# Gated delta rule in a post-norm decoder layer: another order for the slabs' projections, decays, values, key products and block steps

## The chip, the cores and the metric

One core of a Trainium2 chip runs the whole layer in one launch. The metric is device microseconds (us) of one execution, as the median of several runs. All data is float32.

## The reference, cut to what matters

The layer has three parts, each followed by a residual sum and a layer norm: a gated delta rule over 1024 tokens, a cross-attention over 77 context tokens, and a mixture of 8 experts. Batch 4, width 256. The change touches the delta rule alone, which has 4 heads with keys of 64 and values of 128:

```python
normed = (x - mu) * rsqrt(var + EPS) * ln_w + ln_b
q = causal_conv_silu(normed @ Wq, conv_q)     # k and v alike; 4 taps
beta = sigmoid(normed @ Wb)
g = -exp(A_log) * softplus(normed @ Wa + dt_bias)
q = l2norm(q) * HK ** (-0.5); k = l2norm(k)
def _step(S, inp):                            # over the 1024 tokens
    q_t, k_t, v_t, g_t, b_t = inp
    S = S * exp(g_t)
    v_eff = (v_t - einsum('bhk,bhkv->bhv', k_t, S)) * b_t
    S = S + k_t[..., None] * v_eff[..., None, :]
    o_t = einsum('bhk,bhkv->bhv', q_t, S)
o = o * rsqrt(mean(o * o) + EPS) * norm_w
o = o * g_out * sigmoid(g_out)                # g_out = normed @ Wg
return x + o @ Wo
```

## The kernel before

**Slabs.** The 1024 tokens are cut into 8 slabs of 128 tokens, each for all 4 batch rows. Inside a slab the recurrence is solved as a triangular system: a 128 x 128 matrix per batch row and head (16 in all), inverted, then applied to the values and to the state carried from the slab before. A slab passes through these generators and functions:

- `project` (L274): loads the slab's x (`xi`, L277), normalizes and transposes it into `nT` (L300, L304), forms beta and the decay exponent g (matmuls `pb` L317, then some twenty tiny VectorE operations L331 to L353), projects and convolves four 128-wide chunks of q and k (`convolve`, L251: matmuls L257, one ScalarE operation L267, three VectorE ones L269, in two halves, then a Silu L272), sums their squares (L362, `pss` L365, `psst` L377) and turns the cumulated decays into factors (`pd` L384, Exp L393).
- `values` (L414): the same `convolve` for four chunks of v.
- `prepare` (L422), one per batch row: GpSimd spreads g over a mask (L426), a matmul cumulates it (`pe` L432), Exp (L433), GpSimd masks it (L434), the key products `pk` (L444), and VectorE multiplies both into the matrices `bp` (L455).
- `blocks` (L464): the 32 x 32 diagonal blocks of `bp` go through DRAM to a layout with one block per partition (DMAs L477 and L480), are inverted by 31 steps of two VectorE operations each (L488 and L494), and go back through DRAM into `tt` (L498, L503).
- `invert` (L505), one per two batch rows: builds the whole inverse from the blocks (`pw` L513, `pl` L523, `pu` L539 and L546, `pl` L555, `pu` L560).
- `scan` (L564), one per batch row: transposes (L573, L576, L597), the solve and the state (`pwt` L606, `py` L624 and L632, `po` L646 and L654, `pst` L664, L673), the output's norm and gate (L681 to L701, `pg` L690), the output projection (`pot` L705, `px` L711), and the residual and layer norm (L714 to L721).

**Order.** The generators yield where they would wait. `interleave` (L191) takes one section of each in turn, and that sets the order of the program. The framework then orders each engine's instructions by this order and by when its own model finds them ready. Each engine runs its list in that order; tiles come from pools with a fixed number of buffers, PSUM from one pool of 8 banks. For slab i + 1 the loop does:

```python
    for i in range(NS - 1):
        prepared(i + 1)
        ahead = project(i + 2, made[i + 2]) if i + 2 < NS else iter(())
        interleave(*scans(i), chain(values(made[i + 1]), islice(ahead, 9)))
        interleave(*inverts(i + 1), ahead)
```

`prepared` (L732) runs the four `prepare` in two chains and then `blocks`. So the scans of slab i have the values of slab i + 1 beside them and then the first 9 sections of the projection of slab i + 2; the inversion of slab i + 1 has the rest of that projection; `prepare` has nothing beside it. All 31 steps of `blocks` stand in the program ahead of the scans.

Of the kernel before, what the change touches and what calls it, by code (L numbers as in the profile page):

```python
# [2 lines left out]

# [1 line left out]

# [98 lines left out]
def kernel(ctx: ExitStack, tc: tile.TileContext, a: dict, out: bass.AP):  # L104
# [5 lines left out]

    const = ctx.enter_context(tc.tile_pool(name="const", bufs=1))
    banks = ExitStack()
    ps_pool = [banks.enter_context(tc.tile_pool(name="ps", bufs=8, space=PSUM))]

    def bank(name, tag="bank", bufs=None):
        kw = {} if bufs is None else {"bufs": bufs}
# [128 lines left out]
    for j in range(4):  # L245
        z = wp.tile([P, H, P], F32, tag=f"pad{j}", name=f"pad{j}")
        nc.vector.memset(z, 0.0)
        padded.append(z)
    before = []

    def convolve(dst, c, nT):  # L251

        w0 = C_CONV + c * KCONV
        for j in range(2):
            pp = bank("pp")
            for kc in range(KC):
                mm(  # L257
                    pp[:, 0 : 2 * (HALO + P)],
                    lhsT=wqkv[:, kc, c * P : (c + 1) * P],
                    rhs=nT[:, kc, 2 * j : 2 * j + 2, :].rearrange("p b t -> p (b t)"),  # L260
                    start=kc == 0,
                    stop=kc == KC - 1,
                )
            yield
            pre = pp[:, 0 : 2 * (HALO + P)].rearrange("p (b t) -> p b t", b=2)
            ch = dst[:, 2 * j : 2 * j + 2, :]
            nc.scalar.activation(ch, pre[:, :, 0:P], AF.Identity, scale=cols[:, w0 : w0 + 1])  # L267
            for n in range(1, KCONV):
                nc.vector.scalar_tensor_tensor(  # L269
                    ch, pre[:, :, n : n + P], cols[:, w0 + n : w0 + n + 1], ch, ALU.mult, ALU.add  # L270
                )
        nc.scalar.activation(dst, dst, AF.Silu)  # L272

    def project(i, made):  # L274

        made["x"] = xi = slab.tile([P, B, D], F32, tag="xi", name="xi", bufs=3)
        nc.sync.dma_start(out=xi, in_=tokens(i, a["x"]))  # L277
# [75 lines left out]
        nc.vector.tensor_scalar_max(g, g, -1e30)  # L353


        kq = [slab.tile([P, 2, B, P], F32, tag=f"kq{r}", name="kq", bufs=3) for r in range(2)]
        pss = bank("pss")
        for r in range(2):
            for n in range(2):
                yield from convolve(kq[r][:, n], (1 - n) * 2 + r, nT)  # L360
                sqr = wk.tile([P, B, P], F32, tag="sqr", name="sqr", bufs=3)
                nc.scalar.activation(sqr, kq[r][:, n], AF.Square)  # L362
                yield
                o = N_ROWS + (2 * r + n) * 2 * H
                mm(  # L365
                    pss[0 : 2 * H, :],
                    lhsT=nw[:, o : o + 2 * H],
                    rhs=sqr.rearrange("p b t -> p (b t)"),
                    start=r == 0 and n == 0,
                    stop=r == 1 and n == 1,  # L370
                )
# [6 lines left out]
                pss[:, b * 2 * H : (b + 1) * 2 * H], ssT[0 : 2 * H, b, :], ident[0 : 2 * H, 0 : 2 * H]  # L378
            )
        yield  # L380

        pd = bank("pd")
        for n, m in enumerate((le, gt, ones)):
            mm(  # L384
                pd[:, n * B * H : (n + 1) * B * H],
                lhsT=m,
                rhs=g.rearrange("p b h -> p (b h)"),
                start=True,
                stop=True,
            )  # L390
        yield
        ex = slab.tile([P, 3, B, H], F32, tag="ex", name="ex")
        nc.scalar.activation(ex.rearrange("p n b h -> p (n b h)"), pd[:, 0 : 3 * B * H], AF.Exp)  # L393
        el = slab.tile([P, B, 2], F32, tag="el", name="el")
        whole = ex[:, 2].rearrange("p b (r q) -> p b r q", q=2)
        for par in range(2):
            h0 = par * HK
            nc.vector.tensor_copy(el[h0 : h0 + HK], whole[h0 : h0 + HK, :, :, par])

        qw = slab.tile([P, B, 2, H], F32, tag="qw", name="qw")  # L400
        nc.vector.tensor_copy(qw[:, :, 0, :], ex[:, 0])
        nc.vector.tensor_scalar_mul(qw[:, :, 1, :], ex[:, 0], -1.0)

        eq, rk, ik, nb, cd = (small(n) for n in ("eq", "rk", "ik", "nb", "cd"))
        both = pss[:, 0 : 2 * B * H].rearrange("p (b n h) -> p n b h", n=2, b=B)
# [3 lines left out]
        nc.gpsimd.tensor_tensor(ik, ik, bc(phalf.unsqueeze(2), [P, B, H]), ALU.pow)  # L409
        nc.vector.scalar_tensor_tensor(nb, beta, -1.0, rk, ALU.mult, ALU.mult)  # L410
        nc.vector.scalar_tensor_tensor(cd, ex[:, 1], -1.0, nb, ALU.mult, ALU.mult)
        made.update(nT=nT, kq=kq, g=g, nb=nb, cd=cd, ik=ik, eq=eq, el=el, qw=qw)

    def values(made):  # L414
        made["v"] = v = [slab.tile([P, B, P], F32, tag=f"v{c}", name="v", bufs=2) for c in range(H)]
        for c in range(H):
            yield from convolve(v[c], NQK + c, made["nT"])

    def work(name, shape, **kw):
        return wk.tile(shape, F32, tag=name, name=name, **kw)  # L420

    def prepare(i, b, made):  # L422

        g, kq = made["g"], made["kq"]
        ee = work("ee", [P, H, 2, P])
        nc.gpsimd.tensor_tensor(  # L426
            ee[:, :, 1, :], bc(le.unsqueeze(1), [P, H, P]), bc(g[:, b, :].unsqueeze(2), [P, H, P]), ALU.mult
        )
        yield

        pe = bank("pe")
        mm(pe, lhsT=gt, rhs=ee[:, :, 1, :], start=True, stop=True)  # L432
        nc.scalar.activation(ee[:, :, 0, :], pe.rearrange("p (h t) -> p h t", h=H), AF.Exp)  # L433
        nc.gpsimd.tensor_tensor(  # L434
            ee[:, :, 1, :], ee[:, :, 0, :], bc(nge.unsqueeze(1), [P, H, P]), ALU.mult
        )
        yield

        bp = made["bp"]
        pks = [bank("pk") for par in range(2)]  # L440
        for r in range(2):
            for par, pk in enumerate(pks):
                h0 = slice(par * HK, (par + 1) * HK)
                mm(  # L444
                    pk[:, r * 2 * P : (r + 1) * 2 * P],
                    lhsT=kq[r][h0, 0, b, :],
                    rhs=kq[r][h0, :, b, :],
                    start=True,
                    stop=True,
                )  # L450
# [12 lines left out]

    def blocks(i, made):  # L464

        n = NQ * B * H
        mine = slice((i % 2) * n, (i % 2 + 1) * n)

        def diagonal(x, j):
            return x[j * Q : (j + 1) * Q, :, j * Q : (j + 1) * Q]  # L470

        def kept(x, j):
            r0 = (i % 2) * n + j * B * H
            return x[r0 : r0 + B * H, :].rearrange("h (s t) -> s h t", s=Q)

        for j in range(NQ):
            nc.sync.dma_start(out=kept(ab, j), in_=diagonal(made["bp"][:, 0], j))  # L477
        am = slab.tile([P, Q, Q], F32, tag="am", name="am", bufs=1)
        for half in range(2):
            nc.sync.dma_start(  # L480
                out=am[half * n : (half + 1) * n].rearrange("p s t -> p (s t)"), in_=ab[mine, :]
            )
        ut = slab.tile([P, Q // 2, Q], F32, tag="ut", name="ut", bufs=1)
        pr = slab.tile([P, Q // 2, Q], F32, tag="pr", name="pr", bufs=1)
        nc.sync.dma_start(out=ut.rearrange("p r t -> p (r t)"), in_=a["narrow"][:, N_UNIT:])
        for k in range(Q - 1):
# [7 lines left out]
            nc.vector.tensor_tensor(  # L494
                ut[:, :r, k + 1 :], ut[:, :r, k + 1 :], pr[:, :r, :w], ALU.add
            )
        for half in range(2):
# [231 lines left out]
        nc.gpsimd.memset(tt, 0.0)  # L729
        tts.append(tt)  # L730

    def prepared(i):  # L732
# [3 lines left out]
        interleave(*(chain(*gens[n::2]) for n in range(2)))  # L736
        blocks(i, made[i])

    def inverts(i):
        return [invert(b, made[i]) for b in range(0, B, 2)]  # L740
# [3 lines left out]
            chain(scan(i, b, made[i]), scan(i, b + 1, made[i])) for b in range(0, B, 2)  # L744
        ]

    interleave(project(0, made[0]))
    prepared(0)
    interleave(values(made[0]), project(1, made[1]))
    interleave(*inverts(0))  # L750
    for i in range(NS - 1):
        prepared(i + 1)
        ahead = project(i + 2, made[i + 2]) if i + 2 < NS else iter(())
        interleave(*scans(i), chain(values(made[i + 1]), islice(ahead, 9)))
        interleave(*inverts(i + 1), ahead)
    proj_scope.close()
    w_scope = ExitStack()
    xkv = w_scope.enter_context(tc.tile_pool(name="xkv", bufs=1, side="right"))
# [687 lines left out]
```

## Time and profile before

| | |
|---|---|
| median of 3 runs | 1990.59 us (1987.02 to 1990.92) |
| the profiled execution | 1989.58 us, of which the span is 1987.8 us |
| delta rule in the span | 0 to about 877 us |
| first transposes of the scans of slabs 0, 4, 5, 6, 7 (L573) | 140.1, 554.2, 657.6, 761.1, 827.1 us |
| TensorE, VectorE, ScalarE, GpSimd busy in one such distance (450.7 to 554.2) | 89.5, 66.6, 53.5, 24.5 of 103.5 us |
| granted TensorE clock, whole span | 0.909 |

How to read what follows: PE is TensorE (a float32 matmul of this kernel shows as two records), PEld its weight loads, DVE VectorE, ACT ScalarE, POOL GpSimd, SP the engine that issues most DMAs. PEclk is the granted clock of TensorE as a share of full speed. In the view of windows a row is one stretch of the span: its length, then each engine's busy time with its count of instructions, then PEclk, the DMA engines' share and GB/s. In a timeline a row is start, length, engine, line, operation, output and inputs, count, and in brackets the idle time before it and what ended it.

### The profile page before, as it was taken

How to read it: one execution, taken by the hardware profiler on the slowest of the kernel's cores; microseconds unless marked ns; L12 is line 12 of the kernel's file. 1: busy time of each engine (PE TensorE's matmuls, PEld its weight loads, DVE VectorE, ACT ScalarE, POOL GpSimd, SP SyncE). 2: the span in 40 equal slices, each digit the busy share in tenths (PEclk: the TensorE clock that was granted, in tenths of full speed). 3: DMA queues.
4: the chain of work that ended last, by engine and by line, in shares of the span. 5: the costliest groups of instructions: out<-in, count | busy, mean ns of one | idle time of the engine just before them, and what ended most of it. 6: DMA issues, size and time to landing. Idle time of an engine off the chain costs nothing.

```text
span 1987.8 us, 27920 instructions
## 1 busy us (share of the span) xinstructions
PE 1640.0 (83%) x9524; PEld 1163.7 (59%) x9524; DVE 1119.5 (56%) x3199; ACT 918.3 (46%) x2161; POOL 549.5 (28%) x503
## 2 busy tenths in 40 slices
PE   4678898979898888878899999999739999999900
PEld 2456575747575666744676777767616666666600
DVE  4748584857576767434466666566534444444444
ACT  3435463636464545332687776766412222222212
POOL 2222222131222222132345545555410000000065
PEclk9879898989898999789999999999869999999955
DMA  3011010110101011030401100100162111111144
GB/s 113 17 32 23 20 35 17 28 27 22 32 22 33 22 22 44 17 113 0 169 12 33 42 23 32 43 33 22 33 239 77 46 46 46 48 43 48 32 147 136
DMA packets 118347, 98.97 MB, mean 50 GB/s; under 512 B 57803, under 2 KB 106303, under 8 KB 117951
## 3 DMA queue, kind: packets, MB, share of 16 engines
q1 hardware_dynamic: 107135, 75.66, 13.0%
q0 software_dynamic: 6144, 16.79, 2.7%
q10 hardware_dynamic: 4928, 4.74, 0.7%
q8 instruction: 78, 1.28, 0.3%
q14 instruction: 62, 0.51, 0.1%
HBM read 62.12 MB, written 35.03 MB: 49 GB/s over the span
## 4 chain that ended last, share of the span: by engine, by line
PE 49%; DVE 22%; ACT 11%; POOL 8%; issue 5%; DMA 5%; SPq 0%; ACTq 0%; POOLq 0%; DVEq 0%
PE pgt L1299 6%; PE pup L1299 6%; PE pdn L1326 6%; ACT sc L1006 4%; PE pp L257 3%; DMA part<-yg,found 2%; DVE kq L269 2%; DVE v L269 2%; PE pe L432 2%; PE pxo L1040 2%; PE pss L365 2%; DVE bp L455 2%; DVE ut L494 2%; PE pmh L1317 2%; POOL xg L1145 2%
## 5 line engine op out<-in xcount | busy, mean ns | idle before, releaser
L1006 ACT ACTIVATE sc<-sc,ntop,rq 128x77 f32<-128x77 f32 x512 | 182.2, 440 | 71.0 <-DVE ntop L1004 48.2
L1352 POOL DMA_INDIRECT part<-yg,found x64 | 61.3, 958 | 454.7 <-issue 443.7
L1040 PE MATMUL pxo<-vo,aT 128*128 128x256 f32 (+1 forms) x640 | 168.4, 396 | 3.7 <-ACT aT L1025 2.8
L1308 ACT ACTIVATE sge<-sge 128x512 f32<-128x512 f32 x71 | 44.7, 630 | 247.8 <-DVE sge L1307 247.8
L257 PE MATMUL pp<-nT,wqkv 128*128 128x262 f32 x512 | 143.3, 413 | 0.0
L1299 PE MATMUL pgt<-wall,mxT 128*128 x284 | 135.5, 600 | 1.8 <-ACT mxT L1288 1.8
L1299 PE MATMUL pup<-wall,mxT 128*128 x284 | 134.8, 597 | 0.0
L1326 PE MATMUL pdn<-wdn,mhT 128*128 x568 | 134.2, 379 | 0.0
L1040 PEld LDWEIGHTS pxo<-vo,aT 128*128 128x128 f32 (+1 forms) x640 | 117.9, 199 | 21.5 <-ACT aT L1025 5.8
L963 POOL TENSOR_TENSOR rq<-rq,nhalf 128x8 f32<-128x8 f32 x64 | 106.0, 1656 | 76.1 <-DVE rq L962 73.5
L949 PE MATMUL pq<-xwq,xT 128*128 128x512 f32 x256 | 123.0, 603 | 0.5 <-ACT xT L943 0.5
L1011 POOL TENSOR_TENSOR sc<-sc,den 128x616 f32<-128x616 f32 x64 | 77.9, 1218 | 160.7 <-DVE den L1010 77.6
L269 DVE SCALAR_TENSOR_TENSOR v<-pp,cols,v 128x256 f32<-128x256 f32 x192 | 91.3, 476 | 43.9 <-ACT v L267 42.0
L269 DVE SCALAR_TENSOR_TENSOR kq<-pp,cols,kq 128x256 f32<-128x256 f32 x192 | 90.5, 478 | 45.3 <-ACT kq L267 42.8
L257 PEld LDWEIGHTS pp<-nT,wqkv 128*128 128x128 f32 x512 | 96.1, 201 | 33.2 <-issue 16.8
L989 PE MATMUL psc<-kbd,qT 128*128 128x154 f32 x512 | 93.0, 305 | 27.1 <-DVE sc L996 21.9
L1307 DVE TENSOR_TENSOR sge<-pgt,ball 128x512 f32<-128x512 f32 x71 | 49.1, 692 | 112.9 <-PE pgt L1299 112.9
L1326 PEld LDWEIGHTS pdn<-wdn,mhT 128*128 128x128 f32 x568 | 102.5, 190 | 11.0
L685 POOL TENSOR_TENSOR so<-so,nhalf 128x4 f32<-128x4 f32 x32 | 32.4, 1011 | 276.0 <-DVE so L684 276.0
L989 PEld LDWEIGHTS psc<-kbd,qT 128*128 128x128 f32 x512 | 74.6, 196 | 43.3 <-DVE sc L996 30.1
L1299 PEld LDWEIGHTS pup<-wall,mxT 128*128 128x128 f32 x284 | 54.6, 192 | 69.0 <-issue 69.0
L455 DVE SCALAR_TENSOR_TENSOR bp<-pk,nb,ee 128x256 f32<-128x256 f32 x128 | 51.7, 476 | 69.9 <-PE pk L444 40.0
(285 smaller groups left out, 3700.8 us busy)
## 6 DMA issues: line engine op xcount, KB each, us to landing
yg<-my SPq DMA_DIRECT2D x71, 128.0 KB, 1.7
mx<-xg SPq DMA_DIRECT2D x67, 128.0 KB, 2.0
xs<-xd SPq DMA_DIRECT2D x13, 512.0 KB, 4.5
xi<-in_x SPq DMA_DIRECT2D x8, 512.0 KB, 4.1
am<-ab SPq DMA_DIRECT2D x16, 256.0 KB, 4.0
xd<-kd SPq DMA_DIRECT2D x32, 128.0 KB, 2.4
wall<-in_L_ffn_gate_w SPq DMA_DIRECT2D x8, 512.0 KB, 10.5
wall<-in_L_ffn_up_w SPq DMA_DIRECT2D x8, 512.0 KB, 10.8
```

Of the source, the lines that this page charges most:

```text
L257: mm(pp[:, 0 : 2 * (HALO + P)], lhsT=wqkv[:, kc, c * P : (c + 1) * P], rhs=nT[:, kc, 2 * j : 2 * j + 2, :].rearrange("p b t -> p (b t)"), ...
L269: nc.vector.scalar_tensor_tensor(ch, pre[:, :, n : n + P], cols[:, w0 + n : w0 + n + 1], ch, ALU.mult, ALU.add)
L455: nc.vector.scalar_tensor_tensor(bp[:, :, b * H + h], pk[:, r * 2 * P : (r + 1) * 2 * P].rearrange("p (n t) -> p n t", n=2), made["nb"][:, ...
L949: mm(pq, lhsT=t["xT"][:, kc, :], rhs=xwq[:, kc, c0 : c0 + HH * XD], start=kc == 0, stop=kc == KC - 1,)
L963: nc.gpsimd.tensor_tensor(rq, rq, nhalf[:, :HH], ALU.pow)
L989: mm(ps[:, c * 2 * SC : (c + 1) * 2 * SC], lhsT=qT[:, 2 * g + c, :], rhs=kbd[:, half * XC // 2 + 2 * g + c, b, :], start=True, stop=True,)
L1006: nc.scalar.activation(sc[:, h], sc[:, h], AF.Exp, scale=rq[:, h : h + 1], bias=ntop[:, h : h + 1])
L1011: nc.gpsimd.tensor_tensor(sc, sc, bc(den.unsqueeze(2), [P, HH, SC]), ALU.mult)
L1040: mm(px[:, 0:D], lhsT=aT[:w, c, :], rhs=vo[:w, b, half * NV + c, :], start=half == 0 and c == 0, stop=half == 1 and c == NV - 1,)
L1299: mm(ps, lhsT=t["xT"][:, c, :], rhs=wall[:, bass.ds(e * EW + off + c * FF, FF)], start=c == 0, stop=c == KC - 1,)
L1326: mm(px[:, 0:D], lhsT=t["hT"][:, f, :], rhs=wdn[:, bass.ds(e * EV + f * D, D)], start=f == 0, stop=f == FC - 1,)
L1352: nc.gpsimd.indirect_dma_start(out=g, out_offset=None, in_=yg, in_offset=bass.IndirectOffsetOnAxis(ap=found[:, i, b, k : k + 1], axis=0),)
```

## The change

The diff, cut to its core:

```diff
-    ps_pool = [banks.enter_context(tc.tile_pool(name="ps", bufs=8, space=PSUM))]
+    ps_pool = [banks.enter_context(tc.tile_pool(name="ps", bufs=7, space=PSUM))]
...
-    before = []
+    before, exps = [], []
     def convolve(dst, c, nT):
...
-        nc.scalar.activation(dst, dst, AF.Silu)
-    def project(i, made):
+    def decays(i, made):
         made["x"] = xi = slab.tile([P, B, D], F32, tag="xi", name="xi", bufs=3)
...
+        pd = bank("pd")
...
+        ex = slab.tile([P, 3, B, H], F32, tag="ex", name="ex")
+        exps.append(
+            nc.scalar.activation(ex.rearrange("p n b h -> p (n b h)"), pd[:, 0 : 3 * B * H], AF.Exp)
+        )
...
+    def project(i, made):
+        nT, beta, ex = made["nT"], made["beta"], made["ex"]
         kq = [slab.tile([P, 2, B, P], F32, tag=f"kq{r}", name="kq", bufs=3) for r in range(2)]
-        pss = bank("pss")
+        pss = bank("pss", "pss", 1)
         for r in range(2):
             for n in range(2):
                 yield from convolve(kq[r][:, n], (1 - n) * 2 + r, nT)
+                nc.scalar.activation(kq[r][:, n], kq[r][:, n], AF.Silu)
...
     def values(made):
         for c in range(H):
             yield from convolve(v[c], NQK + c, made["nT"])
+        with ExitStack() as behind:
+            for e in exps:
+                behind.enter_context(tc.issue_after(e.ins))
+            exps.clear()
+            for c in range(H):
+                nc.scalar.activation(v[c], v[c], AF.Silu)
...
     def prepare(i, b, made):
-        nc.scalar.activation(ee[:, :, 0, :], pe.rearrange("p (h t) -> p h t", h=H), AF.Exp)
+        exps.append(
+            nc.scalar.activation(ee[:, :, 0, :], pe.rearrange("p (h t) -> p h t", h=H), AF.Exp)
+        )
...
     def blocks(i, made):
         nc.sync.dma_start(out=ut.rearrange("p r t -> p (r t)"), in_=a["narrow"][:, N_UNIT:])
+        yield
+        yield
         for k in range(Q - 1):
...
+            if k % 3 == 2:
+                yield
...
-    for i in range(NS - 1):
-        prepared(i + 1)
-        ahead = project(i + 2, made[i + 2]) if i + 2 < NS else iter(())
-        interleave(*scans(i), chain(values(made[i + 1]), islice(ahead, 9)))
-        interleave(*inverts(i + 1), ahead)
+    interleave(decays(0, made[0]))
+    interleave(project(0, made[0]), decays(1, made[1]))
+    interleave(*prepares(0))
+    interleave(blocks(0, made[0]), project(1, made[1]))
+    for i in range(NS):
+        gens = [*inverts(i)]
+        if i + 1 < NS:
+            gens += prepares(i + 1)
+        if i + 2 < NS:
+            gens.append(decays(i + 2, made[i + 2]))
+        interleave(*gens, values(made[i]))
+        gens = [blocks(i + 1, made[i + 1])] if i + 1 < NS else []
+        if i + 2 < NS:
+            gens.append(project(i + 2, made[i + 2]))
+        if i + 1 < NS:
+            interleave(*gens, *scans(i))
```

`project` is cut in two. `decays` has its first part (x, the norm, beta, g) and the cumulated decays (`pd`, `ex`); the new `project` has the convolutions of q and k and their sums of squares. A turn of the loop now has two stretches. In the first, the inversion of slab i runs beside the key products of slab i + 1, the decays of slab i + 2 and the values of slab i, in this order within each round. In the second, the steps of `blocks` of slab i + 1 and the projection of slab i + 2 run beside the scans of slab i; both stand ahead of the scans in each round, and `blocks` has become a generator that yields twice after its loads and then after every third step. The Silus of the four chunks of v come together at the end of `values`, and `issue_after` puts them on ScalarE's list behind every Exp of the decays and key products traced since the last time (an order of issue, no wait). The sums of squares `pss` get a PSUM bank of their own; the other tiles share 7 instead of 8. The arithmetic stays the same.

More of the change, by code (lines that the diff above doesn't have):

```diff
@@ L1 @@
 from contextlib import ExitStack
-from itertools import chain, islice
+from itertools import chain
 import numpy as np
@@ L353, in project @@
         nc.vector.tensor_scalar_max(g, g, -1e30)
+        pd = bank("pd")
+        for n, m in enumerate((le, gt, ones)):
+            mm(
+                pd[:, n * B * H : (n + 1) * B * H],
+                lhsT=m,
+                rhs=g.rearrange("p b h -> p (b h)"),
+                start=True,
+                stop=True,
+            )
[4 more added lines that the diff above has]
+        )
+        el = slab.tile([P, B, 2], F32, tag="el", name="el")
+        whole = ex[:, 2].rearrange("p b (r q) -> p b r q", q=2)
+        for par in range(2):
+            h0 = par * HK
+            nc.vector.tensor_copy(el[h0 : h0 + HK], whole[h0 : h0 + HK, :, :, par])
+        qw = slab.tile([P, B, 2, H], F32, tag="qw", name="qw")
+        nc.vector.tensor_copy(qw[:, :, 0, :], ex[:, 0])
+        nc.vector.tensor_scalar_mul(qw[:, :, 1, :], ex[:, 0], -1.0)
+        made.update(nT=nT, g=g, beta=beta, ex=ex, el=el, qw=qw)
+    def project(i, made):
+        nT, beta, ex = made["nT"], made["beta"], made["ex"]
         kq = [slab.tile([P, 2, B, P], F32, tag=f"kq{r}", name="kq", bufs=3) for r in range(2)]
-        pss = bank("pss")
+        pss = bank("pss", "pss", 1)
         for r in range(2):
@@ L380, in project, with small @@
         yield
[L382 to L402, printed above, removed]
+        def small(name):
+            return slab.tile([P, B, H], F32, tag=name, name=name)
         eq, rk, ik, nb, cd = (small(n) for n in ("eq", "rk", "ik", "nb", "cd"))
@@ L411, in project @@
         nc.vector.scalar_tensor_tensor(cd, ex[:, 1], -1.0, nb, ALU.mult, ALU.mult)
-        made.update(nT=nT, kq=kq, g=g, nb=nb, cd=cd, ik=ik, eq=eq, el=el, qw=qw)
+        made.update(kq=kq, nb=nb, cd=cd, ik=ik, eq=eq)
     def values(made):
@@ L432, in prepare @@
         mm(pe, lhsT=gt, rhs=ee[:, :, 1, :], start=True, stop=True)
-        nc.scalar.activation(ee[:, :, 0, :], pe.rearrange("p (h t) -> p h t", h=H), AF.Exp)
+        exps.append(
+            nc.scalar.activation(ee[:, :, 0, :], pe.rearrange("p (h t) -> p h t", h=H), AF.Exp)
+        )
         nc.gpsimd.tensor_tensor(
@@ L496, in blocks @@
             )
+            if k % 3 == 2:
+                yield
         for half in range(2):
@@ L730, with prepares @@
         tts.append(tt)
-    def prepared(i):
+    def prepares(i):
         made[i]["bp"] = slab.tile([P, 2, B * H, P], F32, tag="bp", name="bp", bufs=2)
@@ L735, in prepared @@
         gens = [prepare(i, b, made[i]) for b in range(B)]
-        interleave(*(chain(*gens[n::2]) for n in range(2)))
-        blocks(i, made[i])
+        return [chain(*gens[n::2]) for n in range(2)]
     def inverts(i):
@@ L745, in scans @@
         ]
[L747 to L750, printed above, removed]
-    for i in range(NS - 1):
-        prepared(i + 1)
-        ahead = project(i + 2, made[i + 2]) if i + 2 < NS else iter(())
-        interleave(*scans(i), chain(values(made[i + 1]), islice(ahead, 9)))
-        interleave(*inverts(i + 1), ahead)
+    interleave(decays(0, made[0]))
[14 more added lines that the diff above has]
+            interleave(*gens, *scans(i))
     proj_scope.close()
```

## The prediction

> **What bounds the kernel now.** I read the page first: engines, slices, the chain of work that ended last.
>
> ```profile
> PE 1640.0 (83%) x9524; PEld 1163.7 (59%) x9524; DVE 1119.5 (56%) x3199; ACT 918.3 (46%) x2161; POOL 549.5 (28%) x503
> PE   4678898979898888878899999999739999999900
> PEclk9879898989898999789999999999869999999955
> PE 49%; DVE 22%; ACT 11%; POOL 8%; issue 5%; DMA 5%; SPq 0%; ACTq 0%; POOLq 0%; DVEq 0%
> ```
>
> TensorE is the busiest engine, but in slices 1 to 18, the delta rule, it falls to 8 and 7 and its clock to 7 and 8, which it does not in the experts behind. VectorE holds 22% of the chain. So the delta rule is TensorE work broken by waits. The distance between the scans of one slab and the next is 103.5 us six times over (140.1 to 761.1). The view of windows cuts one of them at 515.4 and 554.2, where the inversion and the scans begin, and adds two stretches from the end:
>
> ```profile
> 515.40:554.20 38.80, 30.87 (x313) 18.51 (x311) 19.95 (x59) 16.67 (x32) 11.58 (x9) 0.82 0.08 22
> 554.20:618.90 64.70, 58.57 (x377) 45.90 (x376) 48.65 (x164) 37.90 (x92) 12.95 (x15) 0.97 0.14 30
> 761.10:809.50 48.40, 43.57 (x288) 34.76 (x286) 37.66 (x122) 26.56 (x64) 10.55 (x11) 1.00 0.16 45
> 827.10:877.00 49.90, 44.97 (x298) 35.14 (x296) 16.16 (x44) 24.23 (x67) 10.70 (x11) 0.95 0.03 7
> ```
>
> The second column is TensorE's busy time. The stretch of inversion and key products (38.8 us) is the poor one, at clock 0.82. TensorE's timeline shows where:
>
> ```profile
> 529.46 1.15 PE L257 MATMUL pp<-nT,wqkv 128*128 128x262 f32 x4
> 535.49 1.88 PE L365 MATMUL pss<-sqr,nw 128*8 128x512 f32 x2 [4.88 <-ACT sqr L362]
> 538.03 0.59 PE L377 MATMUL psst<-sq,ssT 8*128 8x8 f32 x4 [0.67 <-ACT ssT L374]
> 538.55 1.46 PE L384 MATMUL pd<-g,sq 128*128 128x16 f32 x6
> 539.85 3.76 PE L432 MATMUL pe<-ee,sq 128*128 128x512 f32 x4
> 543.54 2.99 PE L444 MATMUL pk<-kq 64*128 64x256 f32 x16
> 548.61 3.64 PE L432 MATMUL pe<-ee,sq 128*128 128x512 f32 x4 [2.08 <-POOL ee L426]
> ```
>
> From 530.5 TensorE waits 4.88 us for the projection's tail, then runs at half speed (PEclk 0.50 from 536 to 544): four `pe` records take 3.76 us, where the start of the span, at clock 1.00, shows 1.89. Then GpSimd and VectorE hold it in `prepare`.
>
> **The work at full clock.** From start-to-start distances at clock 1.00, per slab: scans 40.6 us (transposes L573 and L576 3.6; L597 and L606 3.8; `py` 7.1; `po` and `pst` 10.1; `pg` 6.9; `pot` 2.2; `px` 6.9); v convolutions 7.15 (32 records at 0.89 per four); q and k the same; `pss` and `psst` 4.3; inversion 8.7; key products 7.8 (`pe` 3.8, `pk` 4.0); decays 3.4. Together 79.1 us of 103.5. The 38.8 us hold 24.1 of it (inversion, key products, half the q and k convolutions, 3/4 of `pss`, `psst`, `pd`), so TensorE is filled to 62%. The 64.7 us hold 55.0: 85%. Scans with values alone, 761.1 to 809.5, hold 47.75 in 48.4: 98%. The inversion with convolutions beside it (515.4 to 530.5) holds about 14.7 in 15.1: 97%.
>
> **The change, part by part.** No arithmetic is removed; two stretches are filled anew.
>
> First stretch, TensorE: inversion 8.7 + key products 7.8 + decays 3.4 + values 7.15 = 27.0 us. VectorE: inversion 5.2, `bp` 16 x 0.40 = 6.4, decays 6.2, values 24 x 0.40 = 9.6: 27.4. The 10.5 us between 530.5 and 543.6 in which the projection's tail stood alone go, since that tail now lies beside the scans, and `prepare`'s GpSimd products (8 x 1.04 to 1.27 us) have matmuls beside them. What is late next is VectorE, as full as TensorE, and the decays' chain, since the load of x waits for a buffer that the scans before release last (L714): DMA 4.1, statistics 1.8, power 1.0, four normalizations 2.1, transposes and `nT` 2.1, `pb` 1.7, some twenty tiny VectorE operations with an Exp 3.8, `pd` 1.0, Exp 0.2: 17.8 us. Behind its Exp come the table load (1.28) and four Silus (2.1), and behind those `pv` and `vt` of the scans: 21.2 us, covered by 27 while nothing stretches it; each us beyond some 30 counts in full. The floor is 27.4; the ceiling is today's 38.8, as nothing is added to its chain but VectorE work. Between fills of 62% and 97% I take the middle, 80%: 27.0 / 0.80 = **34 us**.
>
> GpSimd's products now run beside the decays' tiny operations. The trace shows such a pair:
>
> ```profile
> 574.28 1.27 POOL L701 TENSOR_TENSOR og<-og,sqr 128x512 f32<-128x512 f32 x1 [1.06 <-ACT sqr L698]
> 574.43 1.20 DVE L494 TENSOR_TENSOR ut<-ut,pr 128x56 f32<-128x56 f32 x1
> ```
>
> The VectorE operation, 0.21 us elsewhere, took 1.20 us and ended with GpSimd's; so did L348 (1.06 against 0.17). Eight products can cost 0 to 8 us; I take 2, since the `bp` and convolution rows keep 0.40 us beside GpSimd, and they are within the 34.
>
> Seven shared banks instead of eight, and six generators in turn: the first stretch asks for 36 banks in 34 us. From 515.4 to 530.5 it was 16 in 15.1 us, `pss` holding one of the eight, at 97% fill and clock 1.00. So the banks cost 0; if every `pk` had to wait for `bp`, about 5 us (two rounds of 2.4), kept for the range. A rule speaks against this: the Trainium skill, "TensorE: Matmul & The Clock Gate", section "A second HAM failure mode: psum-queue depth-cycling", reports that going through the PSUM banks can leave small gaps that throttle the clock again and again. At half clock throughout, the 27.0 us would be 54, and nothing would be gained; the row at clock 1.00 speaks for the other side, and I follow it.
>
> ScalarE changes tables four times a period (1.28 us each, at L272, L330, L698, L393). The Silus behind the Exps leave two. That saves 2.6 us of an engine that is busy 53.5 of 103.5: 0 to 2.6 on the path, counted 0. The Trainium skill, "ScalarE: Activation LUTs", section "What ACT_TABLE_LOAD costs", adds a drain of 1.38 us to each, which would make it 5.3 us. Here the Silu starts at once:
>
> ```profile
> 564.68 1.28 ACT L272 ACT_TABLE_LOAD   x1
> 565.97 0.63 ACT L272 ACTIVATE v<-v 128x512 f32<-128x512 f32 x1
> ```
>
> Second stretch, TensorE: scans 40.6 + projection 11.4 = 52.0 us. VectorE: block steps 17.0, convolutions 9.6, scans 16.6: 43.2. The projection takes the place of the values as filler, with a Square, `pss` and `psst` more; its tail, bare today, has the later scans beside it. Its cover ends with its 14th section of 17 rounds, so the scans' own tail (`og`, `pot`, `px`; 3.4 us idle between 501.8 and 507) stays. The last scans, with no filler at all, take 49.9: that and 52.0 / 0.98 = 53 are floors. Between 85% and 98% I take 91%: **57 us**.
>
> The block steps keep their number. Three every round from the third puts the last into round 13 of 17, some 44 us in; the loads land at about 13, so they do not bind. After the last step, before slab 7, it took 7.8 us until `pw` (L494 at 805.3, `pw` at 813.1): 52 us, 5 before the stretch ends. SP's list carries the same DMAs; a late store of blocks would hold the loads of x and the stores of results behind it (2.0 us at 809.15). Cost 0, up to 3 us.
>
> **The sum.** A period is 34 + 57 = 91 us: six times 12.5 = 75 us less. At the start, today's scans of slab 0 begin 26 us after `pw` (114.1 to 140.1); now a whole first stretch stands there, 36 us from a cold clock: +10. At the end the values of slab 7 (7.15 us) and their Silus lie beside an inversion that takes 14.0 us for 8.7 of work: +5; the key products of slab 7 have no decays beside them: -2. All: -62 us. On the profiled execution, 1989.58 us, that is 1927.6; on the median, 1.0 above it, **1928.6 us**.
>
> **Rivals.** *The scans wait behind the filler (slower).* Convolutions and block steps now stand ahead of the scans in every round, and VectorE takes its list in order. Were all of their 26.6 us to land on the scans' chain, the second stretch would be 49.9 + 26.6 = 76.5, the period 110.5, the time 1990.6 + 42 + 13 = 2046. It decides from a period of 101.3, a second stretch of 67.3: two thirds of the 26.6. For it: at 481.58 and 586.86 TensorE waits 1.44 us for VectorE's `qk`, with block steps around. Against it: from 761.1 to 809.5 VectorE did all 62 steps and 24 convolution operations in 48.4 us, and TensorE lost nothing.
>
> *The first stretch, or the blocks, eat a part.* If the decays' chain or VectorE keeps the first stretch at 38.8 (or the blocks come 5 us too late), the period is 95.8, the time 1990.6 - 46 + 13 = 1958. For it: in the old order that chain took from 521.4 to 532.1 for its statistics alone, since its operations stood last. Against it: it had no use to hurry there.
>
> *It does not do what it says.* If the order planned leaves TensorE's waits where they are, 1990. Against it: TensorE's list follows the program's rounds in the stretch of the inversion.
>
> *Better filled.* At 97% in both, but VectorE's 27.4 + 2 in the first: 29.4 + 53 = 82.4, the time 1990.6 - 127 + 13 = 1877.
>
> **How the numbers follow.** The forecast, periods from 86 to 97 (1899 to 1965), 0.50; a part eaten 0.18; better 0.08; no effect 0.06; slower 0.18. Within 0.2% is about what a measurement of this kernel can tell from no change. Faster 0.76, same 0.06, slower 0.18. The range from 1880 to 1995 leaves out half of the better case and most of the slower one.
>
> **What would show it.** Right: scans of successive slabs (L573) begin some 91 us apart; no idle time of 4.88 us at `pss`; `pe` near 1.9 us per four; PEclk 0.95 or more; two table loads a period; `pw` waiting for no DMA. Wrong: a first stretch above 39 us with VectorE full or `pv` waiting for Silus; TensorE waiting for `qk`, state or `og` behind L269 and L488; TensorE waiting for banks, its clock near 0.7.

## The result, and the profile after

The changed kernel takes **2043.74 us** (median of 4 runs, 2040.71 to 2045.66) against 1990.76 us of the kernel before (4 runs, 1987.02 to 1993.76): a ratio of **1.0265**, 95% interval 1.0249 to 1.0281. It is slower by 53 us; forecast were 62 us less. The profiled execution took 2045.66 us with a span of 2043.9 us. Line numbers below are those of the kernel that each line comes from; the change has moved them (the scans' first transposes: L573 before, L596 after).

The page of the changed kernel, the same four rows as in the prediction:

```profile
PE 1649.7 (81%) x9524; PEld 1177.9 (58%) x9524; DVE 1123.3 (55%) x3199; ACT 905.3 (44%) x2149; POOL 549.8 (27%) x503
PE   4569697878878798886989999999829999999910
PEclk9869798888979699998999999999959999999965
PE 52%; DVE 19%; ACT 9%; POOL 8%; DMA 6%; issue 5%; SPq 0%; ACTq 0%; POOLq 0%; DVEq 0%
```

VectorE's share of the chain fell from 22% to 19%, as wished, and TensorE's rose from 49% to 52%; but in the slices of the delta rule TensorE's busy share still alternates between 6 and 9 tenths. The scans of successive slabs now begin at 156.55, 270.24, 382.80, 495.48, 608.11, 720.72, 807.59 and 879.29 us. (In the table of the kernel before, two of these times are put too late: TensorE's timeline has the first L573 of slab 5 at 657.11 and that of slab 6 at 755.62, not 761.1, so there were five periods of 103.4 us on average and one of 98.5.) The difference of 56.1 us between the spans is made up thus: the start +16.5 (156.55 against 140.06); five full periods of 112.8 us instead of 103.4, +47.1; the period from slab 5 to slab 6, 86.9 against 98.5, -11.6; the last one, 71.7 against 71.5, +0.2; what follows, +3.9.

The view of windows, cut again where the inversion (`pw`) and the scans begin: a full turn of the loop, and then the turn in which slab 6 is inverted. The columns are length, busy time of PE, PEld, DVE, ACT and POOL with counts, PEclk, DMA share, GB/s.

```profile
558.87:608.11 49.24, 36.55 (x347) 27.38 (x346) 25.60 (x82) 18.80 (x35) 10.16 (x10) 0.72 0.06 17
608.11:671.51 63.40, 54.61 (x337) 39.93 (x336) 42.40 (x139) 33.29 (x85) 14.38 (x14) 0.97 0.14 30
783.97:807.59 23.62, 23.44 (x313) 17.86 (x312) 18.06 (x45) 13.64 (x25) 8.04 (x8) 1.00 0.04 13
807.59:862.10 54.51, 47.20 (x298) 36.33 (x297) 33.26 (x112) 25.33 (x69) 10.28 (x11) 0.91 0.15 30
```

The first stretch takes 49.2 us, where the forecast had 34 and a ceiling of 38.8. The second takes 63.4 where it had 57. The third row is the key: it is the same first stretch without the decays, since there is no slab 8, and it takes 23.6 us at clock 1.00 with TensorE busy for 23.4. That is the 27.0 us of the prediction less the 3.4 of the decays, filled to 99%. So neither seven shared banks, nor the values as filler, nor VectorE's work without the decays slow this stretch. What slows it comes with the decays.

TensorE's timeline in the full first stretch shows where; in brackets is the idle time before, and who ended it:

```profile
558.87 1.91 PE L536 MATMUL pw<-sq,tt 128*128 128x128 f32 x16
568.66 0.48 PE L299 MATMUL pt<-sq,nrm 128*128 128x128 f32 x1 [7.88 <-ACT nrm L292]
573.30 3.78 PE L449 MATMUL pe<-ee,sq 128*128 128x512 f32 x4
591.37 1.44 PE L357 MATMUL pd<-g,sq 128*128 128x16 f32 x6 [4.82 <-DVE g L352]
594.67 3.67 PE L583 MATMUL pu<-tt,wt 64*64 64x64 f32 x32
598.27 3.46 PE L449 MATMUL pe<-ee,sq 128*128 128x512 f32 x4
```

Behind the first 16 `pw` stands `pt`, the decays' transposes, and TensorE waits 7.88 us for it. Convolutions of v (L257), the next step of the inversion (`pl`) and the first key products (`pe`) stand behind it on the same list; the copies of `pw` that `pl` reads ended at 561.3, and TensorE runs through all of these without a gap as soon as `pt` is there. Later the same happens once more at `pd`, 4.82 us. After each wait four `pe` take 3.5 to 3.8 us; at full clock, at 122.76 in the same trace, they take 1.99. The chain of work that ended last, at the same place, names what the first wait waits for:

```profile
559.38 0.42 DVE kd L737
...
560.51 4.19 DMA xi<-in_x
...
566.76 1.02 POOL rs L187
...
568.01 0.61 ACT nrm L292
...
568.66 0.48 PE pt L299
```

L737 is the residual sum at the very end of the scans of the slab three before; it is the last reader of one of the three buffers `xi`. The load of x cannot start until it is done, and the program has put the use of that load at the head of the next stretch. The first turn of the loop shows the same list without that cause, since its buffer of x has never been used before: there `pt` follows `pw` without a wait, and the first stretch (116.97 to 156.55) takes 39.6 us, with the wait at `pd` alone.

```profile
120.22 0.60 PE L299 MATMUL pt<-sq,nrm 128*128 128x128 f32 x4
```

The windows between these waits show the clock:

```profile
558.87:560.80 1.93, 1.91 (x17) 1.67 (x15) 1.50 (x5) 1.07 (x2) 0.40 (x1) 1.00 0.00 0
568.66:577.00 8.34, 8.34 (x77) 5.03 (x78) 2.29 (x5) 4.92 (x8) 0.91 (x1) 0.50 0.01 2
578.50:585.00 6.50, 6.50 (x142) 5.55 (x142) 5.47 (x13) 2.10 (x6) 1.10 (x2) 1.00 0.01 3
591.37:601.00 9.63, 9.63 (x46) 7.09 (x47) 3.31 (x9) 1.28 (x3) 0.00 (x0) 0.50 0.01 2
602.50:608.11 5.61, 5.61 (x33) 4.56 (x33) 4.28 (x11) 4.10 (x7) 2.25 (x2) 1.00 0.00 1
```

After each wait TensorE works without a gap at clock 0.50, over the 8.3 and 9.6 us of these rows. So the excess of the stretch over its 27.0 us of work, 22.2 us, is the two waits (7.88 + 4.82 = 12.7) and the half clock behind them (busy 36.55 less 27.0, 9.5).

In the second stretch one wait in the scans' tail has grown: at `pot` TensorE waited 1.61 us before (at 503.44), and now 2.87. GpSimd's timeline and TensorE's show it:

```profile
547.70 2.90 POOL L419 TENSOR_TENSOR ik<-ik,phalf 128x16 f32<-128x16 f32 x1 [1.25 <-DVE rk L418]
550.55 1.26 POOL L724 TENSOR_TENSOR og<-og,sqr 128x512 f32<-128x512 f32 x1
551.87 0.66 PE L728 MATMUL pot<-sq,og 128*128 128x128 f32 x4 [2.87 <-POOL og L724]
553.96 5.08 PE L734 MATMUL px<-wo,qk 128*128 128x256 f32 x16
```

The projection's square root `ik`, a power on a tiny tile that takes 2.90 us, now stands on GpSimd's list ahead of the scans' gate `og`. TensorE waits for that `og`, and the 16 `px` behind it take 5.08 us instead of the 3.62 of full clock.

### The profile page after: what moved, and what is told of

Its sections match the earlier page's. It is cut to its first block, busy times and chain, and to the rows that moved or that the text cites. A ratio compares the mean times of both kernels' runs of the same rounds, so it can differ in the third digit from the quotient of the medians.

```text
span 2043.9 us, 27909 instructions
## 1 busy us (share of the span) xinstructions
PE 1649.7 (81%) x9524; PEld 1177.9 (58%) x9524; DVE 1123.3 (55%) x3199; ACT 905.3 (44%) x2149; POOL 549.8 (27%) x503
## 4 chain that ended last, share of the span: by engine, by line
PE 52%; DVE 19%; ACT 9%; POOL 8%; DMA 6%; issue 5%; SPq 0%; ACTq 0%; POOLq 0%; DVEq 0%
PE pgt L1330 6%; PE pup L1330 6%; PE pdn L1357 6%; ACT sc L1037 4%; PE pp L257 4%; PE pe L449 2%; DMA part<-yg,found 2%; PE px L734 2%; PE pxo L1071 2%; DVE v L269 2%; DVE bp L474 2%; PE pq L980 2%; DMA xi<-in_x 2%; POOL og L724 2%; PE pmh L1348 2%
## 5 line engine op out<-in xcount | busy, mean ns | idle before, releaser
L257 PE MATMUL pp<-nT,wqkv 128*128 128x262 f32 x512 | 152.4, 430 | 0.2 <-DVE tt L574 0.2
L257 PEld LDWEIGHTS pp<-nT,wqkv 128*128 128x128 f32 x512 | 100.0, 212 | 31.7 <-issue 11.0
L1020 PE MATMUL psc<-kbd,qT 128*128 128x154 f32 x512 | 94.0, 308 | 27.3 <-DVE sc L1027 22.2
L1357 PEld LDWEIGHTS pdn<-wdn,mhT 128*128 128x128 f32 x568 | 102.5, 190 | 11.0
L269 DVE SCALAR_TENSOR_TENSOR v<-pp,cols,v 128x256 f32<-128x256 f32 x192 | 87.0, 478 | 13.4 <-ACT v L267 11.3
L1340 DVE TENSOR_TENSOR pup<-pup,ball 128x512 f32<-128x512 f32 x71 | 49.7, 700 | 73.4 <-PE pup L1330 73.4
```

The costliest lines, as they stand in the source:

```text
L257: mm(pp[:, 0 : 2 * (HALO + P)], lhsT=wqkv[:, kc, c * P : (c + 1) * P], rhs=nT[:, kc, 2 * j : 2 * j + 2, :].rearrange("p b t -> p (b t)"), ...
L269: nc.vector.scalar_tensor_tensor(ch, pre[:, :, n : n + P], cols[:, w0 + n : w0 + n + 1], ch, ALU.mult, ALU.add)
L1020: mm(ps[:, c * 2 * SC : (c + 1) * 2 * SC], lhsT=qT[:, 2 * g + c, :], rhs=kbd[:, half * XC // 2 + 2 * g + c, b, :], start=True, stop=True,)
L1340: nc.vector.tensor_tensor(pu, pu, ball[:, bass.ds(e * FF + B_U, FF)], ALU.add)
L1357: mm(px[:, 0:D], lhsT=t["hT"][:, f, :], rhs=wdn[:, bass.ds(e * EV + f * D, D)], start=f == 0, stop=f == FC - 1,)
```

## The experiments

**The theory** behind them: the first stretch is slow because TensorE's list puts the decays' `pt` and `pd` ahead of the work that should cover their chain, and x, which begins that chain, is loaded too late; a wait costs its length and then some 4 to 5 us of half clock. **The rivals**: the filler ahead of the scans holds them up (the slower rival of the prediction); the Silus gathered at the end of the values, or the block steps in pieces, hold something up.

**An early x, and three parts undone.** In the first kernel the scans load the residual's rows a second time, so that `xi` is free as soon as its own slab is normalized:

```diff
-        made["x"] = xi = slab.tile([P, B, D], F32, tag="xi", name="xi", bufs=3)
+        made["x"] = xi = slab.tile([P, B, D], F32, tag="xi", name="xi", bufs=2)
...
+        xr = slab.tile([P, D], F32, tag="xr", name="xr", bufs=4)
+        nc.sync.dma_start(out=xr, in_=tokens(i, a["x"])[:, b, :])
...
-        nc.vector.scalar_tensor_tensor(x1, made["x"][:, b, :], 2.0, px[:, 0:D], ALU.mult, ALU.add)
+        nc.vector.scalar_tensor_tensor(x1, xr, 2.0, px[:, 0:D], ALU.mult, ALU.add)
```

> The changed kernel, except that the scans load the 128 rows of x for the residual a second time (32 small loads more), so that the buffer of a slab's x is free after its normalization and the load for the decays no longer waits for the end of the scans two slabs before. Theory A (the load of x comes late and TensorE's list has the decays' transposes ahead of the inversion, so it stands idle 7.9 us after the first transposes of the inversion and runs on at half clock): the wait of 7.9 us goes, and most of the half clock behind it; distance between scans 112.6 to about 98 us, time 1950 to 1975. Theory B (the scans wait behind convolutions and block steps on VectorE): no change, 2035 to 2050. Theory C (the Silus of v are held behind the Exps): no more than 2 us a slab, 2030 to 2045.

Measured: 1994.37 us (10 runs), ratio to before 1.0024 (1.0014 to 1.0034). The period falls from 112.6 to 102.5 us. One turn in the view of windows:

```profile
426.61:464.71 38.10, 33.25 (x347) 25.66 (x346) 23.56 (x73) 17.94 (x35) 9.12 (x9) 0.82 0.05 15
464.71:529.39 64.68, 56.05 (x337) 41.35 (x336) 42.23 (x139) 33.39 (x85) 14.39 (x14) 0.95 0.15 34
```

All of the gain lies in the first stretch (49.2 to 38.1 us), and TensorE no longer waits at `pt`. The gain is smaller than expected (1950 to 1975), since `pd` still waits for g, 4.82 us in this turn and 6.46 in the first three. The early x is worth 49 us.

The second kernel puts the scans ahead of the filler in every round:

```diff
-            interleave(*gens, *scans(i))
+            interleave(*scans(i), *gens)
```

> The changed kernel with the scans ahead of the block steps and the projection in each round of the second stretch. Theory A: nothing but a shift, 2035 to 2055, the wait before the decays' transposes still 7 to 8 us. Theory B: the second stretch of 63.4 us gets 5 to 6 us shorter, time about 2005 to 2015. Theory C: no change.

Measured: 2045.2 us (4 runs), ratio 1.0276 (1.0257 to 1.0296), no different from the change. Its second stretch takes 64.7 us, not less than the 63.4, and its `pt` still waits (7.94 us). So the filler ahead of the scans costs nothing here; the rival falls, though its price (2046) is the time that came out.

The third lets the Silus of v come when they are ready; they still stand together:

```diff
-        with ExitStack() as behind:
-            for e in exps:
-                behind.enter_context(tc.issue_after(e.ins))
-            exps.clear()
-            for c in range(H):
-                nc.scalar.activation(v[c], v[c], AF.Silu)
+        for c in range(H):
+            nc.scalar.activation(v[c], v[c], AF.Silu)
```

> The changed kernel without the order that puts the four Silus of v behind every Exp; they still stand together at the end of the values. Theory A: no change within 10 us, as the wait comes at the start of the stretch. Theory B: no change. Theory C: the transposes of v come earlier by 2 to 4 us a slab, time 2015 to 2030; against that stand up to two table loads more a slab (1.28 us each).

Measured: 2044.89 us (4 runs), ratio 1.0279 (1.0261 to 1.0297). Between 380 and 610 us ScalarE loads a table 13 times instead of 4, and nothing changes: the order of the Silus neither harms nor helps while TensorE waits for something else.

The fourth issues the steps of the blocks in one piece:

```diff
-            if k % 3 == 2:
-                yield
```

> The changed kernel with the 31 block steps issued in one piece again (the two yields behind the loads stay). Theory A: within 10 us of 2044, since the inverted blocks land 10 us before the inversion already. Theory B: if the steps in front of the scans cost time, it shows here as well, as all 62 now stand ahead of the scans from the third round on: 2050 to 2070. Theory C: no change.

Measured: 2046.09 us (4 runs), ratio 1.028 (1.0262 to 1.0297). The pieces are not what costs.

**The second wait.** Two more yields ahead of `pd` move it two rounds later, behind other sections; once on top of the early x, once on the change alone:

```diff
+        yield
+        yield
         pd = bank("pd")
```

> The second load of x for the residual, as in the run with x loaded twice (1994.4 us), and two more yields ahead of the decays' matmul pd, so that it stands behind the inversion's last products and the next key products. Theory A, continued (what is left of the loss in the first stretch is pd, which waits 4.82 us in TensorE's list for g, and the half clock of pu and pe behind it): both go, the distance between scans falls from 102.7 to about 94 us, time 1935 to 1950. Rival D (VectorE is full in this stretch, so another wait takes the place of this one at once): 1985 to 2000.

> The changed kernel with the two yields ahead of pd, without the second load of x. Theory A with two waits that add up (late x 49 us, pd 35 us): about 2008 us, with the wait of 7.9 us before the decays' transposes still there. If the late x alone makes pd late, so that pd costs nothing once it has been moved or everything comes later anyway: 2035 to 2045.

Measured on top of the early x: 1958.93 us (4 runs, 1956.73 to 1967.92), ratio 0.9848 (0.9808 to 0.9887), between what the theory and the rival expected; `pd` still waits 3.44 us. On the change alone: 2027.77 us (4 runs), ratio 1.0164 (1.0149 to 1.018), again between the two; there `pt` still waits 7.81 us and `pd` 3.44. The first stretch of each:

```profile
404.75:437.62 32.87, 29.40 (x347) 23.07 (x346) 26.42 (x78) 17.52 (x35) 10.07 (x10) 0.95 0.12 28
435.63:481.80 46.17, 34.92 (x348) 26.28 (x347) 27.91 (x88) 18.38 (x35) 11.12 (x11) 0.78 0.14 35
```

Both waits are real and separate: the early x is worth 49 us, the later `pd` 16, both together 85 (by the ratios to the kernel before, 48, 20 and 83). Why the two give some 15 to 20 more together than singly is open.

**The early x in the kernel before.** To see whether the second load would be a gain in any case, the same edit as in the first experiment was made in the kernel before:

> The kernel before with the second load of x for the residual and nothing else. If the early x helps only where the decays stand beside the inversion: 1985 to 1995, no change. If the old kernel too loses by its late x (its normalizations stood ahead of the last Square of the projection, for which TensorE waited 4.88 us): 1950 to 1975.

Measured: 1983.17 us (9 runs, 1976.78 to 1990.61), ratio 0.996 (0.9939 to 0.9981); its wait at `pss` falls from 4.88 to 3.44 us. That is 7 us against 49. The load itself did not come later by the change: before, too, it started as soon as its buffer was free (515.50, at the end of the scans of slab 3). But the first instruction on TensorE's list that needs it stood beside the next scans, 69 us later:

```profile
584.81 0.60 PE L300 MATMUL pt<-sq,nrm 128*128 128x128 f32 x4
```

In the changed kernel `pt` has its turn right behind the first 16 `pw`, 0.3 us after the load has started (560.78 against 560.51). So the wait comes from the earlier use of the load, which the change made, and not from a later load.

**The power ahead of the gate.** A first try delayed the projection's small operations by three yields, on the early x, and with the later `pd`:

```diff
         yield
+        yield
+        yield
+        yield
         def small(name):
```

> The second load of x, and three more yields ahead of the small operations at the end of the projection, so that GpSimd's power of 2.90 us stands behind the scans' last products og instead of ahead of them. If that power costs the scans' tail its wait (2.86 us at pot, and px at 4.74 instead of 3.62 us): 3 to 4 us a slab, time 1968 to 1978. If the tail is bound otherwise: 1990 to 1998.

> Second load of x, pd two yields later and the projection's small operations three yields later, together. Theory A with both: distance about 90 us, time 1915 to 1930, faster than either kernel. Rival D: 1970 or more.

Measured: 1994.42 us (10 runs), ratio 1.0017 (0.9998 to 1.0036), and 1962.42 us (4 runs, 1954.83 to 1971.49), ratio 0.9864 (0.9813 to 0.9915). Each is the same as without the yields (1968 to 1978 and 1915 to 1930 were expected), and this is inconclusive: in the trace the power (2.90 us, at 515.14) still stands ahead of `og` (518.00), and TensorE still waits 2.86 us at `pot`. The edit did not move what it was to move. A second try, on the early x with the later `pd`, gives the order itself:

```diff
-        nc.gpsimd.tensor_tensor(ik, ik, bc(phalf.unsqueeze(2), [P, B, H]), ALU.pow)
+        with ExitStack() as behind:
+            for e in ogs:
+                behind.enter_context(tc.issue_after(e.ins))
+            ogs.clear()
+            nc.gpsimd.tensor_tensor(ik, ik, bc(phalf.unsqueeze(2), [P, B, H]), ALU.pow)
...
-        nc.gpsimd.tensor_tensor(og, og, sg, ALU.mult)
+        ogs.append(nc.gpsimd.tensor_tensor(og, og, sg, ALU.mult))
```

> The run with x loaded twice and pd two yields later (1958.9 us), with GpSimd's power of the projection (2.90 us) put on its list behind the scans' two products og. In that run it stood ahead of them, TensorE waited 2.86 us for pot and ran px at 4.53 instead of 3.62 us. If the power is what holds the scans' tail: 3 to 4 us a slab, time 1930 to 1942. If the tail is bound by its own chain: 1955 to 1962.

Measured: 1941.43 us (5 runs, 1934.88 to 1946.89), ratio **0.9742** (0.9729 to 0.9756). Its windows:

```profile
393.48:427.47 33.99, 30.52 (x348) 24.05 (x346) 25.36 (x77) 17.52 (x35) 10.09 (x10) 0.90 0.15 34
427.47:485.43 57.96, 52.41 (x337) 38.64 (x336) 41.08 (x134) 33.40 (x86) 13.41 (x13) 1.00 0.12 27
```

The second stretch falls from 63.05 us in the kernel without this edit to 57.96, at clock 1.00; the waits at `pot` at its end are 0.38 and 1.00 us instead of 2.86 and 0.71, and 16 `px` take 3.62 us. So some 5 us of this stretch hung on the place of one 2.90 us instruction on GpSimd's list; the first stretch gives 1.1 of them back (32.87 to 33.99), and the five full periods fall from 96.4 to 92.3 us on average.

**One step further, and the scans first once more**, both on this last kernel. The first has two more yields ahead of `pd`, four in all; the second has the scans ahead of the filler, as in the second experiment.

> The fastest run so far (x twice, pd two yields later, the power behind og) with pd two yields later still. There pd still waits 3.44 us for g, at the end of the first stretch, and a half clock follows it. If that wait is only a matter of place: 2 to 5 us a slab less, ratio to the kernel before about 0.962 instead of 0.974. If the Exp behind pd then holds the Silus of v and with them the scans: ratio 0.975 to 0.99.

> The fastest run so far with the scans ahead of the block steps and the projection in each round of the second stretch. Theory B (convolutions and block steps on VectorE hold the scans), now that the first stretch no longer hides it: second stretch 58 us down to 53 to 55, ratio about 0.96. Theory A, that this order costs nothing: ratio 0.97 to 0.98, second stretch 57 to 60 us.

Measured with the later `pd`: **1922.36 us** (4 runs, 1920.63 to 1923.89), ratio **0.9664** (0.9643 to 0.9685), faster than both kernels. Its windows, and `pd` in TensorE's timeline:

```profile
390.22:419.71 29.49, 27.89 (x347) 21.83 (x346) 24.52 (x73) 16.46 (x33) 10.08 (x10) 1.00 0.09 23
419.71:481.52 61.81, 55.87 (x337) 41.16 (x336) 40.88 (x138) 34.55 (x88) 13.38 (x13) 0.94 0.15 33
```

```profile
417.20 0.81 PE L361 MATMUL pd<-g,sq 128*128 128x16 f32 x6 [1.57 <-DVE g L352]
```

The first stretch is down to 29.5 us for 27.0 us of work, at clock 1.00. Much of this comes back in the second (57.96 to 61.81 us): `pv` now waits 1.70 us for v's Silu at its head, and the clock there is 0.66 from 424.4 to 430.0 us. Over the five full periods the mean falls from 92.3 to 90.5 us. With the scans first: 1953.54 us (4 runs), ratio 0.9821 (0.98 to 0.9843), slower than the same kernel with the filler first. Its second stretch takes 62.4 us, more than the 57 to 60 expected of an order that costs nothing, with waits of 2.09 us at `pqd` for VectorE's `qk` and 1.22 at `pss`. So where the first stretch is mended, the filler ahead of the scans is a gain, of 12 us by the medians and 16 by the ratios to the kernel before, the opposite of what the slower rival said.

## Why the prediction was wrong

**The step that failed** is the cover of the decays' chain: "21.2 us, covered by 27 while nothing stretches it". The chain was seen, and its late load too ("the load of x waits for a buffer that the scans before release last"). What was not asked is where its instructions stand on the engines' lists. 27 us of work cover a chain only if that work comes ahead of the instruction that waits; here `pt` stood behind the first 16 `pw`, and the work behind `pt`. The prediction itself had noted that TensorE's list follows the program's rounds. In place of the cover the stretch shows two waits, 7.88 and 4.82 us, and 9.5 us of half clock behind them: 22.2 us over the 27.0 of work. So "the ceiling is today's 38.8, as nothing is added to its chain but VectorE work" was wrong as well: a load of 4.2 us and the statistics, power and normalization behind it were added, bare. And the cover stretched the chain: from the issue of the load (560.51) to `pt` it took 8.15 us, close to the 7.4 of its terms up to the first normalization, but from there to `pd` 22.7, where the rest of them up to `pd` gives 9: TensorE came to `pb` only at 581.61, through its rounds at half clock, and on VectorE's list seven `bp` (2.83 us at 583.05) stood ahead of the tiny operations and three convolutions between them, so that 7.8 us lay between the end of `pb` and `pd` instead of 3.8. The 34 us did come out (33.99) once x was early, `pd` two rounds later and the power behind the gate, but by luck: that stretch has a wait of 3.44 us and a half clock behind it, which the reckoning with a fill of 80% did not contain, and with `pd` later still the same work takes 29.49.

**The half clock** was left out as a price. The prediction had the row for it (at half speed from 536 to 544 after the 4.88 us wait) and counted it only as something that goes. A new wait of 4.82 us costs 9.7 us, and one of 7.88 costs 12. The view of windows above shows it directly.

**The second stretch**: 57 against 63.4. A queue was missed: SP's list was weighed for what is moved past it, GpSimd's was not. The projection's tail brings its power to where the scans end. With that one instruction behind `og` the stretch takes 57.96 us, and the two together 91.95 us, where the forecast was 91. Even so, one bound behind the 57 was misread. The scans of slab 6 begin at 755.62, so the 47.75 us of work lie in 53.9 us and not in the 48.4 from 761.1 on: a fill of 89%, not 98%. "TensorE lost nothing" there is wrong too: it waited 1.97 us for `qk` (788.35) and 2.8 us in all at `pot`. With 85% and 89% as bounds the same reckoning gives 60 us, and the argument against the slower rival loses its row.

**The sum** took six periods of 103.5 us where there were five and one of 98.5, which overstates the gain by 5 us. The kernel with the power behind the gate has both stretches as forecast, and its profiled execution (1934.88 us, the fastest of its five) is 55 us below that of the kernel before, not 62: its six periods come to 72.4 us less instead of 75 (the last of them has no decays), its last period takes 74.1 us (693.40 to 767.52) against 71.5, and what follows takes 4.9 us more, where +3 was forecast for the whole end.

**The start** was put at +10 and is +16.5; with x early, `pd` later and the power behind `og` the scans of slab 0 begin at 150.27, which is +10.2. The end was put at +5 and -2; the last period is +0.2, and what follows +3.9.

**What held**: seven shared banks cost nothing (the stretch of slab 6 at 23.62 us and clock 1.00; the best kernel's at 29.49 us with all generators). Table loads fell to two a period, at L434 and L451. The blocks were in time: their last step began at 540.46 us, 45 after the scans began (44 forecast), and `pw` at 558.87 waited for no DMA. VectorE beside GpSimd's `og` took 1.33 and 1.24 us for two operations of some 0.28 us (at 520.70 and 522.06), which stayed small. The rule of the skill on going through the PSUM banks ("TensorE: Matmul & The Clock Gate", "A second HAM failure mode: psum-queue depth-cycling") was set aside rightly: in these two stretches the banks go round among five and six generators, and the clock stays at 1.00.

**The rivals**: the slower one gave 2046 and the measurement is 2044, but its mechanism is refuted twice, in the change (no difference with the scans first) and in the mended kernel (slower with the scans first). A number that comes out right shows nothing about its reason. Its chance, 0.18, held all the slower cases, and another mechanism filled it. The nearest to the truth was "the first stretch eats a part", which named the decays' chain but kept the ceiling of 38.8.

## What to carry to other kernels

Cover counts only if it stands ahead of the waiting instruction on the same engine's list: for each instruction that begins or continues a moved chain, write down what is issued before it and when its input can be there, from the buffer that its load waits for on. Do this for every in-order list that the chain passes, GpSimd's tiny operations among them. Price a wait on TensorE at its length and the half clock behind it, here as much again for a wait of 4.8 us. And cut a stretch where it begins by the timeline, not at the last start plus a period: a row that begins 5.5 us late made a fill of 89% look like 98%.

## What the runs showed of the hardware

The half clock lasted longer than expected: after idle times of 7.88 and 4.82 us TensorE, busy without a gap, ran at 0.50 for 8.7 us (568.66 to 577.38) and 9.9 us (591.37 to 601.28) before it was back at 1.00. These ends are worked out from the PEclk of rows of half a microsecond, 0.62 from 577.00 to 577.50 and 0.72 from 601.00 to 601.50.

The same rows show a raster. In the changed kernel the clock drops at 563.74, returns at 577.38, drops at 587.62, returns at 601.28, drops at 666.14, returns at 669.54 and drops at 676.38. The distances are 13.64, 10.24, 13.66, 64.86, 3.40 and 6.84 us: 4, 3, 4, 19, 1 and 2 times 3.41. The kernel before fits the same step (drop 535.36, return 545.60, drop 549.02, return 552.42: 3, 1 and 1). So in these traces a half clock begins and ends only on steps of 3.41 us, and the price of a wait depends on where it falls between them. In the kernel with the power behind the gate the same wait of 3.44 us at `pd` was followed by half clock from 419.26 to 426.10 in one turn, two steps, and from 607.00 to 610.42 in another, one step. In the best kernel the clock stayed at 1.00 after 1.57 us of idleness at `pd`, but two waits close together in its second stretch, of 1.70 and 0.77 us, came with half clock from 426.14 to 432.96.

The Trainium skill, "TensorE: Matmul & The Clock Gate", "What's actually happening", gives a warm-up of some 3.4 us of sustained work; the 8.7 and 9.9 us here differ from it, and the measurement decides. The page's remark that the ramp is under 1% of a typical kernel span does not hold where it recurs: here it is 9.5 of the 49.2 us of the first stretch, and five turns have such a stretch, an estimate of 48 of 2044 us.
